# A decoder layer on one core: the first batch's self- and cross-attention moved to the front of the scheduler's plan

## The chip, the cores and the metric

The kernel runs on one core of a Trainium2 chip. Its engines are TensorE (PE; its weight loads are shown as PEld), VectorE (DVE), ScalarE (ACT), GpSimd (POOL) and SyncE (SP). SP issues the DMAs here, all on one queue. The metric is the device time of one execution in microseconds, taken as the median of several runs.

## The reference

The input x has 16 batches of 512 tokens with 256 channels, in float32; a context of 64 tokens belongs to each batch. Cut to what matters, the layer is:

```python
# self-attention, 16 heads, no softmax: a product of two d x d states for each head
q = x + x @ Wq + bq
k_i = x + x @ Wk[i] + bk[i]; v_i = x + x @ Wv[i] + bv[i]          # i = 0, 1
state = prod_i( k_i^T v_i )                                        # per batch and head
a = layernorm(q @ state) * g + b
x = layernorm(x + a @ Wo + bo)
# cross-attention, 16 heads of 64, over 64 context tokens, with a mask
x = layernorm(x + softmax(q' k'^T / 8) v' @ Wout + b_out)
# eight experts; expert e takes the first 1024 tokens with a weight over zero
w = softmax(x @ router_w^T + router_b)
x = layernorm(x + sum_e w[:, e] * relu(x @ W_inter[e]) @ W_out[e])
```

## The kernel before

**The stages.** The self-attention states are formed from the Gram matrix of x: `gram` (ps_g, ps_gt) and, for each four batches, `key_sums` (ps_ks). For one batch, `self_attention` multiplies the Gram matrix with the key weights (ps_gk), forms the states (ps_s), transposes x, folds the query weights in (ps_m, ps_b), computes the output (ps_o), normalizes and transposes it (ps_zt), projects it (ps_p), normalizes again and transposes the result x1 (ps_t into x1T). I call this self(b).

`context_keys`, `output_weights` and `context_values` run over the context of all batches. ps_kv holds keys or values; the keys are written to `k_dram`. For the values, each of eight rows r is first computed (ps_kv) and then multiplied with the output weights (`times_wout`, ps_vo); the result goes through four `vst` buffers to `vo_dram`, with eight stores for a row. values(0) serves batches 0 to 7, values(1) batches 8 to 15.

`cross_attention`, cross(b), folds the query weights into the keys for two batches at a time (`context_group`: loads of kT and of the mask, then ps_kq), computes four tiles of scores (ps_sim, L814), takes their softmax on VectorE, ScalarE and GpSimd (L820 to L804), and multiplies the transposed probabilities with `vo` (ps_x, L834). `vo` comes back from `vo_dram` in eight chunks, each loaded by four DMAs of 132 KB; six chunks have a buffer at the start. A helper, `load_first`, issues these six as soon as the values of that half of the batches are in the program.

`routing` follows cross(b), and needs values(1) for all batches, the first one included. `experts` runs the eight experts over the first two batches. The other batches' tokens go to a loop behind all this that runs only for tokens the experts still take.

**The order.** All these parts are Python generators, each held in a `Stream`. `weave` (L1010) builds the program: it picks, among the streams that are not waiting, the one with the smallest `time()`, and lets it emit instructions up to its next `yield`. A stream's time is `at + span * spent / total`: `plan(at, span, total)` says where it shall begin and end on a scale of microseconds, and `spent` is the TensorE time of what it has emitted, by the planner's own `Model` (L28). `yield WAIT` makes a stream wait until the model has finished what it emitted; `until(...)` asks again every 0.5 us. If the first in line waits, the next one goes: the plan ranks the streams and never leaves TensorE idle as long as anything is ready in the model. The model counts each DMA as its bytes and a fixed time and does not queue DMAs behind one another after the first 40 us.

The order so made binds TensorE, VectorE, ScalarE and GpSimd (`in_order`, L1029). It does not bind the DMA queue: DMAs can be issued earlier than their place in the program.

The planned times around the change are these: grams 0 to 3 from 0 to 40; context keys, output weights and values(0) from 5 to 105; values(1) from 122.8 (SETUP + 0.1 STEP) over 78. For later batches gram b is due at 115 + (b - 4.8) 78, self(b) at 115 + (b - 1) 78, cross(b) at 115 + 78 b, routing(b) at 115 + 78 (b + 1), and the experts start at 216.4. For b = 0 this puts self(0) at 37 and cross(0) at 115.

self(0) may begin when the four grams, their key sums and the remaining weights ("rb" in `cs`) are in the program; cross(0) when self(0) is through.

Of the kernel before, what the change touches and what calls it, by code (L numbers as in the profile page):

```python
# [116 lines left out]
def decoder_layer(  # L117
# [42 lines left out]
    GB = 2  # L160
# [111 lines left out]
    with ExitStack() as att:  # L272
# [770 lines left out]
        SETUP, STEP = 115.0, 78.0  # L1043
        done, finished = {}, {"states": 0, "cross": 0, "routing": 0}

        def made(*tiles):
            return all(model.made[t.name][0] <= model.free["PE"] for t in tiles)

        def until(ready):
            while not ready():  # L1050
                yield 0.5
# [16 lines left out]

        def all_self_attention():
            for b in range(B):  # L1070
                self_st.plan(SETUP + (b - 1) * STEP, STEP, 16.5)
                yield from until(lambda: b in grams and sums[b // QB][1] and "rb" in cs and made(grams[b], sums[b // QB][1][0]))
                yield from self_attention(b, done)

# [6 lines left out]

        def all_cross_attention():
            for b in range(B):
                cross_st.plan(SETUP + b * STEP, STEP, 28.2 + (0 if b % GB else 4.0))
                yield from until(lambda: b in done)
                yield from cross_attention(b, *done[b])
                finished["cross"] = b + 1
# [25 lines left out]
        context_st = Stream(all_context()).plan(5.0, SETUP - 15.0, 71.0)  # L1113
        context_st.ready = 5.0
        self_st, cross_st = Stream(all_self_attention()), Stream(all_cross_attention())
        routing_st = Stream(all_routing()).plan(SETUP + STEP, STEP, 1.0)
        experts_st = Stream(experts()).plan(SETUP + 1.3 * STEP, (B - 0.1) * STEP, FFN)
        self_st.plan(0.0, SETUP, 16.5)
        cross_st.plan(SETUP, STEP, 28.0)
        traced = nc.cur_bb.bb.instructions  # L1120
        first = len(traced)
        streams += [grams_st, context_st, self_st, cross_st, routing_st, experts_st]
# [89 lines left out]
```

## Time and profile before

| | us |
|---|---|
| median of three runs | 1384.72 (1383.49 to 1386.94) |
| the profiled execution | 1389.4 |
| its span, first to last instruction | 1387.6 |
| granted TensorE clock, mean | 0.994 |
| self(0): first ps_gk; transposes of x1 | 54.7; 127.7 |
| cross(0): ps_kq; first ps_sim; first ps_x | 135.1; 142.5; 188.3 |
| values(0): first ps_vo; first vo load behind it | 79.1; 123.1 |
| values(1): last ps_vo starts | 207.8 |

Times in the lower part are counted from the span's start, in the profiled execution. A row of the profile names the line of the kernel, the engine, the operation, the tile written and the tiles read, the shapes, and the number of instructions. One float32 matmul of the kernel shows as two instructions. In brackets stands the idle time of the engine before a row, and what ended it. A timeline row gives start, duration and the merged instructions; the last instruction's end is modelled and can overlap the next row, so the distance from one start to the next is the better measure of what a group takes.

### The profile page before, as it was taken

Reading aid. Unit: us, or ns where it says so; the run is one execution under the profiler, and the core shown is the slowest. Engines: PE = TensorE matmul, PEld = TensorE weight load, DVE = VectorE, ACT = ScalarE, POOL = GpSimd, SP = SyncE. Lnnn points to the kernel's source line nnn. Section 1 sums busy time; section 2 is a strip of 40 time slices with the busy share of each in tenths; the row PEclk is TensorE's granted clock in tenths of the full one; section 3 lists DMA queues with packets and bytes.
Section 4 is the critical chain, followed back from the end, with each engine's and each line's share of the span. In section 5 each row is a group of like instructions: output and inputs, shape, how many; then the busy total and the mean of one; then the engine's idle time right before and its main releaser. Section 6 shows DMA issues by size and latency. Waiting matters only on the chain.

```text
span 1387.6 us, 24209 instructions
## 1 busy us (share of the span) xinstructions
PE 1365.9 (98%) x9630; PEld 1077.9 (78%) x9630; DVE 850.7 (61%) x1957; ACT 402.2 (29%) x912; POOL 203.7 (15%) x140
## 2 busy tenths in 40 slices
PE   8999999999999999999999999999999999999997
PEld 5766576877878787878878787878888787878686
DVE  2445848466584848475584848475665939484744
ACT  1134224132232314142233323142323323232322
POOL 0001112112020111112020112112020202111200
PEclk9999999999999999999999999999999999999999
DMA  8657775511515153522606053513334061505211
GB/s 260 203 136 191 189 195 163 142 32 42 145 53 150 46 142 106 127 77 52 181 24 164 31 142 106 126 62 77 110 95 123 16 187 46 147 26 126 91 56 40
DMA packets 98372, 153.57 MB, mean 111 GB/s; under 512 B 15560, under 2 KB 70096, under 8 KB 98256
## 3 DMA queue, kind: packets, MB, share of 16 engines
q1 hardware_dynamic: 98256, 151.98, 40.1%
q8 instruction: 78, 1.28, 0.4%
q14 instruction: 38, 0.31, 0.1%
HBM read 114.71 MB, written 37.22 MB: 109 GB/s over the span
## 4 chain that ended last, share of the span: by engine, by line
PE 89%; DVE 5%; DMA 2%; SPq 1%; ACT 1%; issue 1%; ACTq 0%; DVEq 0%
PE ps_x L834 16%; PE ps_sim L814 15%; PE ps_e L963 15%; PE ps_h L946 15%; PE ps_gk L629 4%; PE ps_p L711 4%; PE ps_o L687 3%; PE ps_kv L437 3%; PE ps_t L233 2%; PE ps_kq L751 2%; PE ps_vo L492 2%; PE ps_s L641 2%; PE ps_g L555 2%; PE ps_zt L700 1%; PE ps_m L670 1%; PE ps_g L560 1%
## 5 line engine op out<-in xcount | busy, mean ns | idle before, releaser
L946 PE MATMUL ps_h<-head_T,wi 128*128 128x256 f32 x1024 | 239.1, 379 | 0.0
L834 PE MATMUL ps_x<-vo,pT 32*128 32x264 f32 x4096 | 234.9, 384 | 3.9 <-DVE pT L804 3.7
L814 PE MATMUL ps_sim<-kq,x1T 128*128 128x512 f32 x512 | 235.0, 593 | 0.0
L834 PEld LDWEIGHTS ps_x<-vo,pT 32*128 32x128 f32 x4096 | 211.5, 186 | 26.1 <-issue 5.6
L946 PEld LDWEIGHTS ps_h<-head_T,wi 128*128 128x128 f32 x1024 | 193.4, 190 | 38.8 <-issue 13.0
L802 POOL TENSOR_TENSOR s<-s,sm 128x1024 f32<-128x1024 f32 x64 | 121.7, 1901 | 539.8 <-DVE sm L801 501.4
L841 DVE TENSOR_TENSOR x<-ps_x,x 128x264 f32<-128x264 f32 x64 | 23.2, 426 | 226.3 <-PE ps_x L834 226.3
L822 ACT ACTIVATE s<-s 128x512 f32<-128x512 f32 x128 | 80.7, 630 | 276.1 <-DVE s L821 276.0
L814 PEld LDWEIGHTS ps_sim<-kq,x1T 128*128 128x128 f32 x512 | 94.5, 190 | 83.2 <-issue 74.5
L820 DVE TENSOR_REDUCE mx<-ps_sim 128x8 f32<-128x512 f32 x128 | 86.1, 673 | 42.0 <-PE ps_sim L814 41.6
L821 DVE TENSOR_TENSOR s<-ps_sim,mx 128x512 f32<-128x512 f32 x128 | 88.5, 692 | 4.4
L725 POOL TENSOR_TENSOR x<-x,bout 128x1056 f32<-128x1056 f32 x16 | 38.7, 2420 | 320.7 <-ACT hT L952 172.6
L804 DVE STREAM_TRANSPOSE pT<-s 128x1024 f32<-128x1024 f32 x64 | 78.6, 1228 | 7.0 <-POOL s L802 7.0
L952 ACT ACTIVATE hT<-ps_h 128x256 f32<-128x256 f32 x128 | 46.9, 376 | 119.9 <-PE ps_h L946 119.8
L701 ACT ACTIVATE zT<-ps_zt,shift,gain 128x512 f32<-128x512 f32 x32 | 23.2, 775 | 189.5 <-PE ps_zt L700 189.5
L800 DVE TENSOR_REDUCE sm<-s 128x16 f32<-128x1024 f32 x64 | 77.1, 1204 | 0.4 <-ACT s L822 0.4
L261 ACT ACTIVATE rstd<-bn_mv,eps 128x4 f32<-128x4 f32 (+1 forms) x70 | 20.7, 295 | 159.5 <-DVE bn_mv L250 156.0
L267 ACT ACTIVATE x<-x,off,rstd 128x264 f32<-128x264 f32 (+1 forms) x112 | 58.3, 591 | 29.3 <-DVE off L265 29.3
L687 PE MATMUL ps_o<-m,xT 128*128 128x264 f32 x256 | 66.7, 387 | 0.0
L954 DVE TENSOR_SCALAR hT<-ps_h 128x256 f32<-128x256 f32 x128 | 52.2, 409 | 22.5 <-PE ps_h L946 22.3
L711 PE MATMUL ps_p<-wo,zT 128*128 128x264 f32 x256 | 63.1, 387 | 0.0
L629 PE MATMUL ps_gk<-wk,g 128*128 128x256 f32 x256 | 61.2, 382 | 0.0
(174 smaller groups left out, 1897.4 us busy)
## 6 DMA issues: line engine op xcount, KB each, us to landing
vo<-vo_dram SPq DMA_DIRECT2D x512, 132.0 KB, 4.2
vo_dram<-vst SPq DMA_DIRECT2D x128, 132.0 KB, 2.4
xt<-in_x_dram SPq DMA_DIRECT2D x16, 512.0 KB, 4.0
wi<-L_ffn_experts_inter_dram SPq DMA_DIRECT2D x8, 1024.0 KB, 5.3
gx<-in_x_dram SPq DMA_DIRECT2D x15, 512.0 KB, 4.2
x_rest<-x SPq DMA_DIRECT2D x14, 512.0 KB, 3.1
out_dram<-x SPq DMA_DIRECT2D x14, 512.0 KB, 2.9
kT<-k_dram SPq DMA_DIRECT2D x8, 512.0 KB, 3.3
```

Of the source, the lines that this page charges most:

```text
L629: nc.tensor.matmul(ps[:, :C], blk, wk[:, j, k, :], start=(j == 0), stop=(j == NC - 1))
L687: nc.tensor.matmul(ps[:, :CX], xT[:, cc, t * P:(t + 1) * P], m[:, cc, :], start=(cc == 0), stop=(cc == NC - 1))
L711: nc.tensor.matmul(ps[:, :CX], zT[:, cc, t * P:(t + 1) * P], wo[:, cc, :], start=(cc == 0), stop=(cc == NC - 1))
L802: nc.gpsimd.tensor_mul(s, s, sm.unsqueeze(2).to_broadcast([P, NH, J]))
L804: nc.vector.transpose(probsT[:, :, t, :], s.rearrange("p h (a j) -> p (h a) j", a=2))
L814: nc.tensor.matmul(ps, x1T[:, cc, t * P:(t + 1) * P], kq[:, cc, hf * 512:(hf + 1) * 512], start=(cc == 0), stop=(cc == NC - 1),)
L820: nc.vector.tensor_reduce(mx[:, hs], sim, AX.X, ALU.max)
L821: nc.vector.tensor_sub(s[:, hs, :], sim, mx[:, hs].unsqueeze(2).to_broadcast([P, 8, J]))
L822: nc.scalar.activation(s[:, hs, :], s[:, hs, :], AF.Exp, scale=SCALE)
L834: nc.tensor.matmul(ps[q][:, :CX], probsT[pq, blk].rearrange("p t i -> p (t i)"), vos[c][pq, i, :], start=(c == 0 and i == 0), stop=(c == 7 ...
L946: nc.tensor.matmul(ps[:, :TB], wi[:, cc, f * P:(f + 1) * P], head_T[b][:, cc, t0 * P:t0 * P + TB], start=(cc == 0), stop=(cc == NC - 1),)
L963: nc.tensor.matmul(ps[:, :C], hT[f][:, t * P:(t + 1) * P], wo_[:, f, :], start=(f == 0), stop=(f == NF - 1),)
```

## The change

In the plan, self-attention and cross-attention of batch 0 get the due time 0 and a span of 0, which they keep until they have finished: their time stays 0 whatever they have spent. From batch 1 on both streams are planned as before. What each part waits for (`until`, WAIT) is untouched, and so are all instructions.

```diff
         def all_self_attention():
             for b in range(B):
-                self_st.plan(SETUP + (b - 1) * STEP, STEP, 16.5)
+                if b > 0:
+                    self_st.plan(SETUP + (b - 1) * STEP, STEP, 16.5)
                 yield from until(lambda: b in grams and sums[b // QB][1] and "rb" in cs and made(grams[b], sums[b // QB][1][0]))
                 yield from self_attention(b, done)
...
         def all_cross_attention():
             for b in range(B):
-                cross_st.plan(SETUP + b * STEP, STEP, 28.2 + (0 if b % GB else 4.0))
+                if b > 0:
+                    cross_st.plan(SETUP + b * STEP, STEP, 28.2 + (0 if b % GB else 4.0))
                 yield from until(lambda: b in done)
                 yield from cross_attention(b, *done[b])
                 finished["cross"] = b + 1
...
         experts_st = Stream(experts()).plan(SETUP + 1.3 * STEP, (B - 0.1) * STEP, FFN)
-        self_st.plan(0.0, SETUP, 16.5)
-        cross_st.plan(SETUP, STEP, 28.0)
+        self_st.plan(0.0, 0.0, 1.0)
+        cross_st.plan(0.0, 0.0, 1.0)
         traced = nc.cur_bb.bb.instructions
```

## The prediction

> **What bounds the kernel now.** I read the shares of busy time first, then the chain of work that ended last, then the windows by stage, then TensorE's timeline with the queue that issues the DMAs beside it. From the page:
>
> ```profile
> PE 1365.9 (98%) x9630; PEld 1077.9 (78%) x9630; DVE 850.7 (61%) x1957; ACT 402.2 (29%) x912; POOL 203.7 (15%) x140
> PE 89%; DVE 5%; DMA 2%; SPq 1%; ACT 1%; issue 1%; ACTq 0%; DVEq 0%
> vo<-vo_dram SPq DMA_DIRECT2D x512, 132.0 KB, 4.2
> ```
>
> TensorE is busy for 98% of the span and carries 89% of the chain: it sets the end. The change removes no matmul and adds none. So it can act only through the time in which TensorE stands still or runs slowly, and through the order in which that time falls. Busy time hides part of this, so I take undisturbed start-to-start distances from the timeline as the work of a group: ps_kv x4 1.72 us (44.26 to 45.98), ps_vo x16 1.98 (79.13 to 81.11), ps_sim x4 1.72, ps_o or ps_p x4 0.89, ps_zt 0.88, ps_m with ps_b 1.34, ps_kq 3.77, a batch's ps_x 14.5. Elapsed time less this work is what I call lost.
>
> ```profile
> 63.50:79.00 15.50, 15.50 (x82) 12.59 (x80) 5.71 (x12) 2.08 (x4) 0.00 (x0) 0.78 0.00 0
> 79.00:123.50 44.50, 43.98 (x221) 27.05 (x221) 24.15 (x64) 19.07 (x47) 2.57 (x3) 1.00 0.85 203
> 123.50:210.00 86.50, 84.55 (x623) 59.05 (x621) 53.79 (x115) 27.23 (x66) 12.51 (x8) 1.00 0.73 186
> ```
>
> Columns: window, its length, busy us of PE, PEld, DVE, ACT, POOL, then the granted clock, the DMA share, GB/s. The first window has a clock of 0.78: its groups add up to 12.0 us of work, so 3.6 are lost to the slow clock. In 79 to 123.7 the groups add up to 39.9 of 44.6, so 4.7 are lost. In 123.7 to 252.7 they add up to 118.0 of 129.0: 11.0 lost. Of those, 5.9 lie around ps_vo of values(1) (0.8, 1.2, 1.3, 1.8 and 0.8) and 1.2 in batch 0's ps_x. Together 19.3 us are lost while the moved work runs; that is all the change has to gain, or to add to.
>
> ```profile
> 54.74 3.62 PE L629 MATMUL ps_gk<-wk,g 128*128 128x256 f32 x16
> 62.60 1.04 PE L233 MATMUL ps_t<-ident,xt 128*128 128x128 f32 x8
> 68.84 3.77 PE L555 MATMUL ps_g<-gx 128*128 128x257 f32 x8
> ...
> 81.11 1.16 PE L670 MATMUL ps_m<-state,wqT 128*128 128x128 f32 x8
> 109.23 2.07 PE L492 MATMUL ps_vo<-xwoutT,st 64*128 64x264 f32 x8 [0.49 <-ACT vst L186]
> 188.26 12.12 PE L834 MATMUL ps_x<-vo,pT 32*128 32x264 f32 x207
> 336.82 15.93 PE L834 MATMUL ps_x<-vo,pT 32*128 32x264 f32 x256 [3.25 <-DVE pT L804]
> ```
>
> The reader is to see where batch 0's attention stands: it starts at 54.74, pauses from 62.60 to 81.11, and reaches ps_x only at 188.26.
>
> **Part 1: self(0) from second place to first.** Its gates (four grams, the key sums, the router bias's load issued) are unchanged, and with a due time of 37 it was already ahead of the grams (40), so its first steps, to 63.5, stay. Then the pause goes: ps_m and ps_b 1.34, ps_o 3.56, ps_zt 0.88, ps_p 3.56 and the transposes of x1 0.88, 10.2 us of TensorE work, run as soon as their inputs are there, with wo, gram 4 and the first ps_kv in their waits. Adding the waits (the norm's moments and four activations about 4 us, twice; zT with POOL's sum about 2), x1T is ready at about 93 instead of 130. What it saves: nothing by itself, since other work filled the pause. The slow clock of 63.5 to 79 comes while groups of 4 and 8 columns stand close together (ps_rw, ps_wo); ps_m and ps_o now lie between them. From 0 to -3.6 us; no row tells which, so I take half, **-1.8**. Cost if the cover is gone: values(0) starts some 4 us later.
>
> **Part 2: cross(0) first.** kT and the mask are loaded long before (the queue issues kT at 58.17), so ps_kq (3.77) runs at about 93, and four tiles of ps_sim (13.75) follow to about 119; VectorE's share, 0.67+0.69 for each of 8 halves, 1.2 for each of 4 sums and 4 transposes, is 20.5 us beside them. This leaves some 5 us for values(0) in that time. By my count four of its eight rows of ps_vo and six of ps_kv are done at 119, and 4x1.98+2x1.72 = 11.4 us of TensorE work remain, which now run **with nothing between them**: self(1) is due at 115, while the context stream's time stays below 105. Here the stores decide:
>
> ```profile
> 117.98 5.04 SPq L497 DMA_DIRECT2D vo_dram<-vst  x8
> 139.15 12.63 SPq L781 DMA_DIRECT2D vo<-vo_dram  x23
> ```
>
> A row of ps_vo issues 8 stores in 5.04 us. Four rows take 20.2, so the last store goes out at about 139, while TensorE could be done at 130. Four vst buffers and eight banks let it run ahead by about 8 us of stores, so I count 3 lost there and 2 beside the softmaxes, 5.0 against the 4.7 of 79 to 123.7: **+0.3**.
>
> **Part 3: ps_x(0), the step that I think decides.** Its 32 vo loads wait for values(0). Before, they were issued from 123 to 152 and needed at 188: 36 us of cover. Now ps_x(0) is first in the plan as soon as the planner believes the loads have landed; it gives each DMA its own bytes and a fixed time and no queue, so some 5 us after values(0) ends. In those 5 us self(1)'s ps_gk fit (3.5), and TensorE reaches ps_x at about 138.7. Queued behind ps_x in TensorE's order are self(1) and values(1): nothing else can fill. The loads stand behind the last stores on SP: first issue 139.5, four issues a chunk at 0.55 (12.63/23) 2.2, landing 4: the first chunk is there at 145.7. Eight chunks at 2.2 against the 1.81 that ps_x needs for one, and the end is at 145.7+7x2.2+1.8 = 162.9 instead of 138.7+14.5 = 153.2: 9.7 lost, 8.5 more than the 1.2 of before. The Trainium skill's page "DMA: Bandwidth & Descriptors" (Specifications) gives a core about 358 GB/s of HBM: 132 KB would take 0.38 us, a chunk 1.5, a row's stores 3.0. By that the stores keep up (row work 3.7), the loads would begin by about 132, and ps_x would wait for no more than a microsecond: -0.2 instead of +8.5. The row shows 0.55 and 0.63 us for such a transfer, so I take the row: **+8.5**, from +1 (loads hoisted among the stores, as kT and one vo load at 123.08 were) to +16 (values(1)'s stores get in between: 16 of them take 10, as they did at 127 to 138). A wait of this length can slow the clock as well: after 3.25 us of idleness batch 2's ps_x took 15.93 instead of 14.5. I leave these 1.4 out, because slow matmuls hide under the chunks' pace.
>
> **Part 4: values(1) loses its neighbour.** From about 163 to the plan's 193 only self(1) (12.5 left), values(1) (28) and gram 5 (2.7) are due: 43 us against 64 stores, 40.3 us. That is the mix of 79 to 123.7, so 4.7 lost instead of 5.9: **-1.2**, from -5.9 to +4.
>
> **Part 5: from 193 on.** The due times of every later batch are the same, and by both sums that point falls near 209 us: moved forward and moved back cancel in TensorE's work (42 us of attention early, as much context and self(1) late). The 1128 us behind it hold few losses, 4.7 at batch 2 (3.25 idle and 1.4 of slow clock) and the tail, untouched. A shift of a few us re-deals such waits: -4.7 to +9, taken as **0**.
>
> Sum: -1.8+0.3+8.5-1.2+0 = **+5.8 us**. On the profiled execution's 1389.4 us (span 1387.6 and 1.8 around it) that is 1395.2. The median of the runs shown, 1384.7, lies 4.7 below the profiled one; the same 5.8 us give **1390.5**.
>
> **Rivals.** *The cover holds* (no change): SP's order is not TensorE's, and chunks that need only the first rows could be loaded among the stores. Part 3 is then about +2, the sum -0.7: 1384. For it: kT issued 77 us before its use. Against it: in the trace vo loads go out only from 123.08, after the last store of values(0).
> *The gain* (faster): values(1) is slowed by the neighbour that moves, 20.5 us of softmax on VectorE and 12.63 us of vo issues between its stores. Without them its 5.9 us at 130 to 188 vanish, and with -1.8 and +0.3 the sum is -7.4 plus what ps_x(0) waits beyond before; below a wait of 7.4 this side wins, and with 2 it gives 1379. For it: ps_vo's waits stand right there. Against it: the stores alone ask for 40 of the 43 us.
> *Later waits* (slower): two more waits like that of batch 2, 9.4 us together, on top of the forecast: 1400. For it: such a wait costs 4.7. Against it: only one of that size is seen in 1128 us.
> That the change does little is possible too: ps_x(0) can't precede values(0), so cross(0) gains at most 50 us; it is in the first rival.
>
> **Chances.** Forecast 0.50, cover holds 0.22, gain 0.18, later waits 0.10. A measurement of this kernel can tell about 0.3%, 4.2 us, from no change. Slower by more: nearly all of the forecast (0.45) and the last, 0.55; within: the rest of the forecast and the first rival, 0.27; faster 0.18. The unknown ends of part 3 and 5 give 1378 to 1403 for 8 in 10; the forecast's own range is 1386 to 1400.
>
> **What would show it.** ps_m follows ps_rw within 3 us, x1T comes near 93, ps_kq near 95; the clock of 63 to 79 tells part 1. In the timeline ps_x(0) starts near 139 to 146 and takes well over 14.5 us, with vo loads right behind the stores; values(1) ends near 209. I am wrong if ps_x(0) takes 15 us or less, if TensorE has filler there, or if the difference arises after 250 us.

## The result, and the profile after

The changed kernel takes 1416.6 us (median of 4 runs, 1416.1 to 1417.7) against 1385.8 before: a ratio of 1.0225, 95% interval 1.0207 to 1.0242, or 31 us more. The profiled spans are 1414.6 and 1387.6, 27 apart: the profiled execution before the change (1389.4 us) was slower than its median, and the stages below account for the 27. Of the runs further down, one execution (self_only, 1793 us at a granted clock of 0.75) was slow and is left out. The forecast of 1390.5 had the sign right and the size of the rise too small by a factor of five.

The page first, with the busy times of the engines and the chain of waits:

```profile
PE 1372.7 (97%) x9630; PEld 1081.4 (76%) x9630; DVE 855.1 (60%) x1957; ACT 402.7 (28%) x912; POOL 203.6 (14%) x140
PE 89%; DVE 5%; DMA 3%; ACT 1%; SPq 1%; issue 1%; ACTq 0%; DVEq 0%
```

As many TensorE instructions as before, 7 us more of them counted as busy, and a span longer by 27: the time went into waits and slow matmuls. The windows of the changed kernel say where (columns as before the change):

```profile
63.50:79.00 15.50, 15.38 (x114) 14.17 (x112) 12.36 (x30) 3.20 (x8) 2.52 (x2) 1.00 0.01 2
79.00:124.00 45.00, 41.95 (x227) 25.68 (x226) 25.61 (x56) 18.97 (x42) 4.31 (x2) 1.00 0.46 121
160.00:210.00 50.00, 47.97 (x357) 33.21 (x356) 21.51 (x54) 16.09 (x40) 2.55 (x3) 0.97 0.82 203
210.00:253.00 43.00, 36.76 (x172) 26.28 (x171) 27.46 (x66) 12.91 (x31) 5.32 (x4) 0.92 0.62 168
253.00:300.00 47.00, 40.26 (x364) 34.07 (x364) 23.55 (x50) 8.15 (x19) 7.21 (x5) 0.93 0.38 93
```

The clock in the first window is full now (0.78 before). The two last windows are the worst, with 6.2 and 6.7 us of idleness and a clock of 0.92 and 0.93. They lie **behind** all the work that was moved, whose last step, ps_x(0), ends at 170.6. TensorE's timeline has the places:

```profile
149.04 2.49 PE L834 MATMUL ps_x<-vo,pT 32*128 32x264 f32 x36
154.03 16.61 PE L834 MATMUL ps_x<-vo,pT 32*128 32x264 f32 x220 [2.50 <-DMA vo<-vo_dram]
...
240.85 2.04 PE L946 MATMUL ps_h<-head_T,wi 128*128 128x256 f32 x4 [5.91 <-issue]
...
273.72 16.23 PE L834 MATMUL ps_x<-vo,pT 32*128 32x264 f32 x256 [6.74 <-DVE pT L804]
...
360.71 17.10 PE L834 MATMUL ps_x<-vo,pT 32*128 32x264 f32 x256 [5.49 <-DVE pT L804]
```

ps_x(0) starts at 149 and takes 21.5 us to the next group instead of 14.5. The experts' first ps_h waits 5.9 us, ps_x(1) 6.7, ps_x(2) 5.5, and the matmuls behind each wait run slowly. From batch 3 on both kernels run alike: ps_x(4) stands at 521.7 here and 494.8 before, ps_x(15) at 1351.2 and 1324.3, 26.9 apart both times.

With the measure of the prediction (elapsed time less the undisturbed work of the groups), the loss by stage is:

| stage | lost before | lost after | difference | forecast |
|---|---|---|---|---|
| up to the transposes of batch 0's x | | | +1.4 | 0 |
| from there to ps_zt(0) (before: to the first ps_vo) | 3.6 | 2.4 | -1.2 | -1.8 |
| values(0), up to ps_x(0) or its old place | 4.7 | 8.1 | +3.4 | +0.3 |
| ps_x(0) | 1.2 | 7.0 | +5.8 | +8.5 |
| values(1), up to the first ps_sim(1) | 8.3 | 6.3 | -2.0 | -1.2 |
| first ps_sim(1) to ps_x(1) | 1.6 | 16.2 | +14.6 | 0 |
| slow clock in ps_x(1); ps_x(2) with its wait | 4.7 | 9.8 | +5.1 | 0 |

The four stages that the prediction worked out add up to +6.0 where it had +5.8. Another 20 us came where it had put a zero; the first 1.4 lie ahead of anything that the change moves.

**Two suspects.** The first is wi, the weights of the experts' first product (ps_h). The queue's timeline of the changed kernel:

```profile
215.33 10.22 SPq L497 DMA_DIRECT2D vo_dram<-vst  x16
225.68 0.50 SPq L299 DMA_DIRECT2D gx<-in_x_dram  x1
226.29 0.50 SPq L611 DMA_DIRECT2D xt<-in_x_dram  x1
226.84 7.64 SPq L781 DMA_DIRECT2D vo<-vo_dram  x11
234.53 0.43 SPq L980 DMA_DIRECT2D wi<-L_ffn_experts_inter_dram  x1
```

The 1 MB of wi is issued at 234.5, behind the last stores of values(1) and eleven loads for ps_x(1), and lands 6.1 us later, at 240.6; ps_h starts at 240.85. Before the change it was issued at 219.4 and needed at 228.2.

The second is VectorE ahead of ps_x(1). First its timeline in the kernel before, then in the changed one; the routing of batch 0 (w_all, rm) stands there in both:

```profile
249.94 0.24 DVE L858 TENSOR_TENSOR w_all<-x_head,rb 128x32 f32<-128x32 f32 x1
250.21 0.19 DVE L859 TENSOR_REDUCE rm<-w_all 128x4 f32<-128x32 f32 x1
250.43 0.19 DVE L860 TENSOR_TENSOR w_all<-w_all,rm 128x32 f32<-128x32 f32 x1
```

```profile
267.82 1.23 DVE L858 TENSOR_TENSOR w_all<-x_head,rb 128x32 f32<-128x32 f32 x1
269.09 0.19 DVE L859 TENSOR_REDUCE rm<-w_all 128x4 f32<-128x32 f32 x1
269.31 2.19 DVE L860 TENSOR_TENSOR w_all<-w_all,rm 128x32 f32<-128x32 f32 x1
271.42 0.15 DVE L265 SCALAR_TENSOR_TENSOR off<-bn_mv,rstd 128x4 f32<-128x4 f32 x1
...
272.34 1.24 DVE L804 STREAM_TRANSPOSE pT<-s 128x1024 f32<-128x1024 f32 x1
```

The same two operations, 32 elements a partition, take 1.23 and 2.19 us instead of 0.24 and 0.19, and the last transposition of the probabilities is queued behind them. GpSimd's timeline in that stretch of the changed kernel:

```profile
267.11 1.90 POOL L802 TENSOR_TENSOR s<-s,sm 128x1024 f32<-128x1024 f32 x1 [4.89 <-DVE sm L801]
268.95 0.21 POOL L704 COPY xt<-z 128x32 f32<-128x32 f32 x1
269.11 2.34 POOL L705 TENSOR_TENSOR xt<-xt,bo 128x1024 f32<-128x1024 f32 x1
```

Each long VectorE operation ends with the GpSimd operation beside it, at 269.0 and at 271.45. The first of the two can't delay the transposition of the probabilities, which needs the result of that GpSimd operation (L802) anyway; the second can.

### The profile page after: what moved, and what is told of

Its sections match the earlier page's. It is cut to its first block, busy times and chain, and to the rows that moved or that the text cites. A ratio compares the mean times of both kernels' runs of the same rounds, so it can differ in the third digit from the quotient of the medians.

```text
span 1414.6 us, 24204 instructions
## 1 busy us (share of the span) xinstructions
PE 1372.7 (97%) x9630; PEld 1081.4 (76%) x9630; DVE 855.1 (60%) x1957; ACT 402.7 (28%) x912; POOL 203.6 (14%) x140
## 4 chain that ended last, share of the span: by engine, by line
PE 89%; DVE 5%; DMA 3%; ACT 1%; SPq 1%; issue 1%; ACTq 0%; DVEq 0%
PE ps_x L834 17%; PE ps_h L946 15%; PE ps_sim L814 15%; PE ps_e L963 14%; PE ps_p L711 4%; PE ps_gk L629 4%; PE ps_kv L437 4%; PE ps_o L687 3%; PE ps_t L233 2%; PE ps_kq L751 2%; PE ps_s L641 2%; PE ps_g L555 1%; PE ps_vo L492 1%; DMA vo_dram<-vst 1%; PE ps_zt L700 1%; PE ps_m L670 1%
## 5 line engine op out<-in xcount | busy, mean ns | idle before, releaser
L834 PE MATMUL ps_x<-vo,pT 32*128 32x264 f32 x4096 | 241.2, 390 | 14.7 <-DVE pT L804 12.2
L946 PE MATMUL ps_h<-head_T,wi 128*128 128x256 f32 x1024 | 241.2, 382 | 5.9 <-issue 5.9
L834 PEld LDWEIGHTS ps_x<-vo,pT 32*128 32x128 f32 x4096 | 214.9, 189 | 40.3 <-issue 16.1
L946 PEld LDWEIGHTS ps_h<-head_T,wi 128*128 128x128 f32 x1024 | 194.8, 191 | 45.7 <-issue 19.8
L802 POOL TENSOR_TENSOR s<-s,sm 128x1024 f32<-128x1024 f32 x64 | 121.7, 1902 | 552.8 <-DVE sm L801 500.4
L437 PE MATMUL ps_kv<-cT,wT 128*128 128x512 f32 x128 | 61.6, 620 | 1.5 <-ACT vst L186 1.3
```

The lines of the kernel that those rows point to most:

```text
L437: nc.tensor.matmul(ps, wT[:, cc, r % 4 * P:(r % 4 + 1) * P], cT[:, cc, q * 512:(q + 1) * 512], start=(cc == 0), stop=(cc == NC - 1),)
L802: nc.gpsimd.tensor_mul(s, s, sm.unsqueeze(2).to_broadcast([P, NH, J]))
L834: nc.tensor.matmul(ps[q][:, :CX], probsT[pq, blk].rearrange("p t i -> p (t i)"), vos[c][pq, i, :], start=(c == 0 and i == 0), stop=(c == 7 ...
L946: nc.tensor.matmul(ps[:, :TB], wi[:, cc, f * P:(f + 1) * P], head_T[b][:, cc, t0 * P:t0 * P + TB], start=(cc == 0), stop=(cc == NC - 1),)
```

## The experiments

### Is wi the head of a chain?

The kernel before reads up to 1.5 us higher in the later runs (1387.3 against 1385.8), so differences of that size between runs are not read here. My first theory joined the two suspects: VectorE stood 7 us behind the first relu, which waited for wi, so the softmax of batch 1 came late. Four runs bear on it.

```diff
                     wo_ = load_outer(e)
+                    yield 8.0
```

> The changed kernel, with the experts' stream held back for 8 us of the planner's time behind the issue of its first weights. Chain theory: the 5.9 us in which TensorE waits for wi and the slow clock behind it (2.9) also hold VectorE behind the first relu (7.0), so that the softmax of batch 1 comes late and ps_x(1) waits 6.7 and runs slowly (1.7); all of it goes: 17 us less, about 1400 us (1397 to 1404), and ps_x(1) waits under 2 us. Rival, two separate losses: ps_x(1) waits because the routing's small VectorE operations of batch 0 stand in its way; then only 8.8 us go, about 1408 us, and ps_x(1) still waits 5 us or more.

1397.9 us, 18.7 less; the wait for wi is gone and ps_x(1) waits 0.76. The number is the chain theory's. But the pause also moved the order: the routing's operation L858 now runs at 233.9, far ahead of ps_x(1). So this run alone can't tell the theories apart; the next two can. It shows one thing more: the routing's last operation, L865, takes 2.30 us at 254.08, directly ahead of the last transposition, and still ps_x(1) hardly waits. A long operation there is not enough to make TensorE wait.

```diff
             yield from until(lambda: len(vos) == 6 and made(*vos))
+            pause = {0: 10.0}
+            if b in pause:
+                yield pause[b]
```

> The changed kernel, with cross(0) held back for 10 us of the planner's time ahead of ps_x(0), so that other work fills TensorE while the vo loads land. Chain theory: ps_x(0) takes 15 to 16 us instead of 21.5, and its 6 us come back, with a part of the wait for wi: 1405 to 1411 us. Rival, ps_x(0) is what sets all later waits: the stores of values(1) go out earlier, wi is in time, and 1395 us or less is reached.

1409.8 us, in the range that was expected, and for another reason than was given. TensorE's timeline of this kernel, in which three added lines make L837 of L834 and L949 of L946:

```profile
162.25 1.25 PE L492 MATMUL ps_vo<-xwoutT,st 64*128 64x264 f32 x2 [5.79 <-ACT vst L186]
163.42 17.00 PE L837 MATMUL ps_x<-vo,pT 32*128 32x264 f32 x256
...
233.13 1.10 PE L949 MATMUL ps_h<-head_T,wi 128*128 128x256 f32 x4 [0.48 <-issue]
...
263.21 16.35 PE L837 MATMUL ps_x<-vo,pT 32*128 32x264 f32 x256 [6.73 <-DVE pT L804]
```

ps_x(0) takes 17.0 and not 15 to 16, and the work put ahead of it waits 5.8 us for its own stores: stores and loads share one queue, 18 vo loads go out from 148.07 on, and the stores behind them only from 157.97. So the pause moved the wait and removed little of it. The wait for wi has gone (0.48). And ps_x(1) still waits 6.73: **the chain theory falls.** The wait ahead of ps_x(1) doesn't need a late wi.

The two halves of the change alone, each with the other stream planned as before:

> Only self(0) at due time 0; cross(0) planned at 115 as before the change. Chain theory: the vo loads of batch 0 are covered again, and values(1) ends near 210; the slow clock of 63 to 79 us is gone: 1382 to 1390 us. Rival, the delay of values(0) by self(0) alone is enough to make wi late: 1400 us or more, with a wait of 4 us or more ahead of the first ps_h.

1407.3 us (ratio 1.0150, 1.0122 to 1.0178), where 1382 to 1390 was expected: a miss for the theory, and the run that taught most. wi is in time (0.6), ps_x(0) takes 14.65 us behind a wait of 2.5, and still ps_x(1) waits 6.74 and ps_x(2) 5.50, with L858 at 1.24 and 1.37 us.

> Only cross(0) at due time 0; self(0) planned at 37 as before the change, so cross(0) starts at about 128 us, behind values(0). Chain theory: ps_x(0) comes near 165 us with its loads landed, values(1) runs behind it without cover and ends a few us later than before: 1386 to 1396 us. Rival, cross(0) at the front is the whole loss: 1405 us or more.

1392.6 us (1.0045, 1.0026 to 1.0064), as expected. L858 takes 0.24 and 0.16 us here, and ps_x(1) waits 0.5.

So the wait of 6.7 us ahead of ps_x(1) doesn't go with wi. It is there when L858 to L865 all stand directly ahead of the last transposition (the changed kernel, x0_pause, self_only), and not when the first of them ran long before (wi_wait) or when L863 to L865 stand behind it (cross_only).

### Moving the routing, in both kernels

Why does the routing stand there at all? Its stream has a total of 1.0 us for a span of 78. For batches 0 and 1 it emits eight transposes, 0.88 us in the planner's model; that moves its time by 78 x 0.88 = 69 us, and its small VectorE operations fall due beside the next batch's ps_x. The experts' second product, ps_e, is held back with them: the program emits it only when the routing of its batch is through (`until(lambda: finished["routing"] > b)`). Later batches have no transposes and no such delay. One number takes this away:

```diff
-                routing_st.plan(SETUP + (b + 1) * STEP, STEP, 1.0)
+                routing_st.plan(SETUP + (b + 1) * STEP, STEP, 100.0)
```

> The changed kernel, with one number of the plan changed: the routing stream's total 100 instead of 1, so that the small VectorE operations of the routing of batches 0 and 1 come right behind the transposes and not 69 us later by the plan, which put them between the last softmax operations of the next batch. Collision theory: there two of them take 1.2 and 2.2 us instead of 0.2 while GpSimd runs a tensor operation, and hold the last transposition of the probabilities back; without them ps_x(1) waits 2.5 us or less instead of 6.7 and ps_x(2) 2 or less instead of 5.5, with the slow clock behind each (1.7 and 2.6): about 12 us less, 1404 us. Rival, TensorE has simply no other work in the plan at these two places: both waits stay within 1.5 us and the time is 1411 us or more.

1399.8 us, 16.8 less than the changed kernel; more than the 12 expected. Both waits are gone entirely. TensorE's timeline of the changed kernel ahead of ps_x(1), then that of this kernel:

```profile
263.37 3.62 PE L963 MATMUL ps_e<-wo__2013,hT 128*128 128x256 f32 x16
```

```profile
241.05 2.05 PE L946 MATMUL ps_h<-head_T,wi 128*128 128x256 f32 x4 [6.52 <-issue]
...
260.84 1.89 PE L963 MATMUL ps_e<-wo__2018,hT 128*128 128x256 f32 x8
...
264.35 5.34 PE L963 MATMUL ps_e<-wo__2018,hT 128*128 128x256 f32 x24
269.80 14.52 PE L834 MATMUL ps_x<-vo,pT 32*128 32x264 f32 x256
...
347.02 14.52 PE L834 MATMUL ps_x<-vo,pT 32*128 32x264 f32 x256
```

wi is as late as in the changed kernel, and ps_x(1) and ps_x(2) follow with no wait and at full speed. That separates the two losses from the other side.

What does the routing do to ps_x(1)? The traces give two effects. In the changed kernel TensorE runs out of work at 267.0. The last transposition could start at 269.0, when L802 ends, and starts at 272.34: the routing's operations cost 3.3 of the 6.74 us (2.0 of them by L860's length). The other 3.4 us are TensorE's own lack of work. With the routing moved, 32 matmuls of ps_e instead of 16 stand ahead of ps_x(1), 3.5 us more, and fill them. No run moves ps_e alone, so this second half is read from the two traces and the program, and not tested by itself.

> The kernel before, with the routing stream's total 100 instead of 1. Collision theory: the wait of 3.25 us ahead of ps_x(2) and the 1.4 of slow clock behind it go: about 4.7 us less, 1381 to 1383 us. Rival, the order has no slack and the moved operations delay another softmax: 1386 us or more.

1381.7 us, against 1386.8 for the kernel before on the same chips: a ratio of 0.9970 (0.9959 to 0.9982). The wait of 3.25 us ahead of ps_x(2) that the kernel before shows is gone, so it came from the routing's place in the plan too. But not from a long operation. VectorE and GpSimd ahead of ps_x(2) in the kernel before:

```profile
333.76 1.68 DVE L865 TENSOR_TENSOR w_all<-w_all,rm 128x32 f32<-128x32 f32 x1
335.43 1.25 DVE L804 STREAM_TRANSPOSE pT<-s 128x1024 f32<-128x1024 f32 x1
333.50 1.90 POOL L802 TENSOR_TENSOR s<-s,sm 128x1024 f32<-128x1024 f32 x1 [8.42 <-DVE ks L590]
```

L865 takes 1.68 us, but it ends with L802 at 335.4, and the transposition needs L802. Its length costs nothing. What differs is again TensorE's work: between the last ps_sim and ps_x(2) stand 16 matmuls of ps_e before, and 32 with the routing moved (12.5 us of work in all against 14.9). This version beats both kernels.

### Is it GpSimd that holds VectorE?

```diff
-            nc.gpsimd.tensor_add(xt[:, :, :C], xt[:, :, :C], cs["bo"].unsqueeze(1).to_broadcast([P, NT, C]))
+            b in (2, 3) or nc.gpsimd.tensor_add(xt[:, :, :C], xt[:, :, :C], cs["bo"].unsqueeze(1).to_broadcast([P, NT, C]))
```

> The changed kernel, with GpSimd's addition of the output bias (L705, 2.34 us) left out for batches 2 and 3 alone, so that part of the sum is missing there; the order of the other engines is the same up to ps_x(2). Shared-access theory: the routing's VectorE operation at L860 took 2.19 us in place of 0.19 because it ran beside that GpSimd operation. Now it takes 0.2 us, while L858, beside another GpSimd operation, stays at 1.2; ps_x(1) starts about 2 us earlier, its wait is 4.4 to 5 us instead of 6.7, and ps_x(2)'s 3.2 to 3.8 instead of 5.5: about 4 to 5 us less in all, 1412 us. Rival, the operation waits for its input: L860 stays near 2.2 us and the waits stay.

GpSimd's addition of a bias is left out for two batches here. 1411.4 us, 5.2 less. The timelines of VectorE, GpSimd and TensorE in this kernel:

```profile
267.89 1.90 POOL L802 TENSOR_TENSOR s<-s,sm 128x1024 f32<-128x1024 f32 x1 [4.89 <-DVE sm L801]
268.60 1.24 DVE L858 TENSOR_TENSOR w_all<-x_head,rb 128x32 f32<-128x32 f32 x1
...
270.09 0.19 DVE L860 TENSOR_TENSOR w_all<-w_all,rm 128x32 f32<-128x32 f32 x1
...
272.50 3.90 PE L834 MATMUL ps_x<-vo,pT 32*128 32x264 f32 x32 [4.74 <-DVE pT L804]
```

L860 is back at 0.19; L858, whose GpSimd neighbour is still there, stays at 1.24; ps_x(1) waits 4.74 and ps_x(2) 3.45. All as expected, with the order of the engines unchanged up to there: the GpSimd operation is the cause of L860's length, and that length is 2.0 us of each wait. The rest of the waits stays, so the collision theory of the expectations holds for that part alone. The page "SBUF — State Buffer" of the Trainium skill (section "SBUF: two separate sides") states it as an exclusive lock: a VectorE operation with two inputs in SBUF and a GpSimd operation that reads SBUF exclude each other, and the second waits for the whole of the first. The traces agree: L858 and L860 have two such inputs and end with the GpSimd operation beside them, while L859, with one, took 0.19 us in the changed kernel although L705 had started beside it (269.11).

### What is left

> The changed kernel with both pauses, 8 us behind the issue of the experts' first weights and 10 us ahead of ps_x(0). Separate losses: what the two gave alone adds up, 1416.6 - 18.7 - 6.8 = 1391 us (1388 to 1394). Rival, they share a cause: with ps_x(0) mended the weights are in time anyway, and the time is 1397 us or more.

1398.4 us (1.0086, 1.0059 to 1.0113): the rival's range. With the pause behind wi in place, the pause ahead of ps_x(0) adds nothing; TensorE waits 5.5 us in ps_vo instead, and ps_x(0) takes 17.6.

> The changed kernel with the routing stream's total 100 and the pause of 8 us behind the issue of the experts' first weights. If the wait for wi is a loss of its own, its 6.5 us and the slow clock behind it (2 to 3) come back on top of the 16.8 of the routing: 1389 to 1393 us. Rival, the pause only helped because it moved the order away from the collision: 1396 us or more.

1390.8 us, 9.0 less than with the routing's number alone, and the first ps_h waits 0.24 instead of 6.52: wi is a loss of its own.

> Only self(0) at the front, with the routing stream's total 100. Collision theory: the 21 us that self(0) alone cost were mostly the collisions at ps_x(1) and ps_x(2); what is left are the 6 us by which values(1) ends later: 1385 to 1391 us. Rival, self(0) at the front costs more than half by itself: 1396 us or more.

1389.4 us (1.0013, 1.0005 to 1.0022 against the kernel before).

> Only cross(0) at the front, with the routing stream's total 100. In the run without it ps_x(1) waited 0.5 and ps_x(2) 3.2 us, like before the change, so the number brings only what it brought to the kernel before, about 5 us: 1386 to 1389 us. Rival: nothing comes back, 1391 us or more.

1386.9 us (0.9996, 0.9981 to 1.0012). With the routing out of the way the parts can be set against 1381.7: self(0) at the front costs 7.7 us, cross(0) 5.2, and both together 18.1, of which 9.0 are the wait for wi.

The last run asked what sets the pace of the stores:

```diff
-                        nc.sync.dma_start(
+                        (nc.scalar if bl else nc.sync).dma_start(
                             out=vo_dram[(q * NG + g) * GB + bl, :, r * 2:(r + 1) * 2, :],
```

> The changed kernel, with half of the stores of vst (the odd batch of each pair) issued by ScalarE instead of SyncE. If SyncE's issue sets the pace of 0.63 us a store, a row of eight takes about 3 us instead of 5, values(1) ends 5 to 10 us earlier and the time falls to 1400 us or less. If the DMA engines set it (their share was 0.80 to 0.97 while stores or loads ran), a row still takes 4.5 us or more by both queues, and the time stays within 6 us of 1416.6.

In between, so undecided. ScalarE issues its four stores of a row at 96.97, 97.97, 98.97 and 99.97, 1.0 us for a pair on the two queues instead of 1.27 on one, or 4.0 us a row. The time, 1408.9, can't be read as the price of the pace: the order changed with it, and ps_x(1) no longer waits (0.8).

## Why the prediction was wrong, step by step

**The sign** was right, but by its own mark ("if the difference arises after 250 us") the forecast was wrong: some 11 of the 27 us arise there, in the waits ahead of ps_x(1) and ps_x(2) and behind them. **Parts 1 to 4** agree in sum (+6.0 against +5.8) by luck, since misses of up to 3.1 us cancel.

- *Part 1, self(0) at the front.* The clock of 63 to 79 rose from 0.78 to 1.00, so the whole 3.6 came back, but ps_wo's evictions and the norm cost 2.4: -1.2. It isn't shown that the new neighbours brought the clock back. In routing_before the same groups stand there in the same order as before the change (ps_rw to ps_kv, 60.84 to 73.17), at a clock of 1.00 and with 0.2 lost; in routing_cross and cross_only they run at 0.78 and 0.89. So the slow clock came and went with the order of the groups unchanged, and what set it stays open. ps_kq at 102 came later than the 93 that I counted.
- *Part 2, values(0).* Mis-sized: 8.1 lost, not 5.0. Waits for vst stand in nearly every row of ps_vo from 88 to 140, beside the softmaxes too, where I had allowed 2.
- *Part 3, ps_x(0).* The mechanism is seen (a wait of 2.5 for vo, loads right behind the stores, 19.3 us for 36 of them, some already ps_x(1)'s); lost 7.0, not 9.7; six loads had slipped in between the stores by 138, which can account for it. What I had not seen is that filling the gap with values(1) doesn't help, because the filler's stores stand in the same queue (x0_pause, both_waits).
- *Part 4, values(1)*: -2.0 against -1.2.

**Part 5 is the step that failed**, as it was put: "The due times of every later batch are the same", "untouched", "taken as 0", with -4.7 to +9. It cost 20 us, for two reasons. (The 1128 us are counted from 252.7, not from 209; nothing rests on that.)

- I priced the 3.25 us ahead of ps_x(2) as a wait that is re-dealt by chance, without asking what it was. It comes from the plan: for two batches the routing's total puts the routing, and with it the release of ps_e, next to the following batch's ps_x (routing_before: the wait goes and the time falls by 5 us). Before the change ps_x(1) waited 0.5 and ps_x(2) 3.25; after it they waited 6.7 and 5.5 (routing_after: both gone, 16.8 us less). Of each of these two, 2.0 us are a VectorE operation held up by GpSimd (no_bo).
- I followed the moved step's DMAs up to ps_x(0) and no further. values(1)'s last ps_vo came at 217.4 instead of 207.8, so the queue reached wi 15 us later, while the experts' due time stayed. The planner doesn't queue DMAs, so it emitted ps_h right behind (routing_wi: 9.0 us). Before the change the slack was below a microsecond: landed at 227.7, used at 228.2.

**The rivals.** "Later waits" named the right place with two waits like batch 2's and the price of 9.4 on top of the forecast, 1400; it lacked the wait for wi and its slow clock, and the size of the two waits. "The gain" and "the cover holds" are refuted: ps_x(0) took 21.5 us.

## What to carry to other kernels

A plan with due times that moves a block early also moves everything that shares its queue later: look for the first consumer *behind* the block whose data come by that queue, and for how many microseconds it has in hand. Before pricing a wait as chance, ask why the waiting engine has nothing else to do there, and which stream holds its work back; here that pointed to a loss that the kernel already had. An operation that takes ten times its usual duration costs only what it adds to the path: 2.0 us at L860, nothing at L858 or, before the change, at L865, which end with a GpSimd operation that the next step needs as well. And a run that meets a theory's number isn't enough when its edit also moves the order; look in the trace whether the link that the theory names is there.

## What the runs showed of the hardware

- A small VectorE operation with two inputs in SBUF took 2.19 us instead of 0.19 while a GpSimd tensor operation of 2.34 us ran, and 0.19 again with that operation left out; the profile counts the wait as VectorE's busy time, so no idle time shows it.
- Behind waits of 5.5 to 6.7 us TensorE ran slowly (granted clock 0.92 and 0.93 in the two windows): ps_x took 16.2 and 17.1 us instead of 14.5, and the three groups behind the wait for wi (ps_h x4, ps_t x8, ps_h x8) took 2.9 us more than usual. In 63 to 79 us the same order of groups was granted a clock of 0.78 (before, routing_cross), 0.89 (cross_only) and 1.00 (routing_before).
- Stores of 132 KB went out every 0.63 us on one queue, and every 0.50 on two in the row at 97 us of two_queues_act.
